# Scaling into SBUF, deviations for four batches, and a new division of work in a conditional adapter

## The chip, the cores and the metric

The kernel runs on one core of a Trainium2 chip. Five engines work side by side, each in the order of its own instructions: TensorE (PE in the profile; PEld is its weight load), VectorE (DVE), ScalarE (ACT), GpSimd (POOL) and SyncE (SP), which here only issues DMA transfers. The metric is the device time of one execution in microseconds, as the median of several runs; lower is better.

## The reference

For each of 128 batches b there are 128 rows of 512 numbers, x[b], and a language v = itok[b], one of 10. All is float32.

```python
w1, w2 = W1[language_ids], W2[language_ids]                 # 512 x 128, 128 x 512
h = relu(einsum('bsh,bha->bsa', x, w1) + b1[language_ids])
y = x + einsum('bsa,bah->bsh', h, w2) + b2[language_ids]
mean = y.mean(-1); var = ((y - mean) ** 2).mean(-1)
out = x + (y - mean) * rsqrt(var + 1e-5) * gamma[language_ids] + beta[language_ids]
```

## The kernel before

A batch is one tile of 128 rows x 512. W2 and the rows of beta, gamma and b2, spread over 128 partitions, stay in SBUF for all languages, and so does W1 in a tile `w1`. Each batch passes through these steps (functions of the same names):

- TensorE turns the four 128 x 128 blocks of x into PSUM (`transpose_x`), and ScalarE copies them to SBUF (`copy_xT`). For some batches ("F" in `TURNS`) x is loaded once more in blocks of 32 columns (`load_blocks`, four transfers), W1 likewise in rows that fit (`load_rows`, four transfers), and VectorE turns the blocks (`turn_blocks`); such a batch needs neither `transpose_x` nor `copy_xT`.
- W1 of the batch's language is copied by ScalarE from `w1` into a tile of its own (`stage_w1`); for "F" and "w" batches it comes by DMA.
- `down` (four matmuls of the program, eight instructions in the trace), `relu` on ScalarE, `up` into a PSUM tile `py`.
- x and b2 are added in one of several ways, by the batch's letter in `KINDS`. "P": GpSimd computes r = x + b2 (`add_b2`), and VectorE adds r to `py`. "E": ScalarE copies x into `py` first (`seed`), `up` accumulates onto it, and VectorE adds b2. A few batches at the beginning take other ways. The VectorE step is `residual`; it also writes the row sums.
- ScalarE squares (`square`), with the sum of squares as a by-product, and makes the negative mean (`scalar_means`) and the reciprocal root (`deviation`); VectorE refines the root in three small Newton steps (`rstd`). Means, roots and Newton steps are made for two batches at once. The root is written to a PSUM tile.
- VectorE scales: `scale` writes (py - mean) x gamma back to `py`, in PSUM. GpSimd has meanwhile written x + beta to the output tile o (`add_beta`). `finish`, the ending, computes o = py x rstd + o on VectorE.
- A pair of batches is stored by one transfer.

PSUM has five tiles for `py`. The output pool has 8 pairs. x is loaded in fours, in 4 buffers.

The order of each engine's instructions is fixed by the program. Batches 0 to 3 and the last five (from `E` on, and parts of the seven before them) are written out by hand. For all others a list `plan` holds each step with a time in units of one batch: the batch's number plus a number from a table (`BATCH` and `PAIR` in the steady part, `BATCH_EDGE` and `EDGE` outside it). The list is sorted by these times, and each engine gets its instructions in that order. In the steady part the letters repeat every 16 batches, a period:

```python
KINDS = 'EPPPPPEPEPPPEPPP'
TURNS = 'TTTTFTTTTwTTFTTT'
```

The lines that the profile names are: L330 `transpose_x`, L334 `copy_xT`, L302 `turn_blocks`, L321 `stage_w1`, L353 `down`, L361 `relu`, L367 and L375 `up`, L340 `add_b2`, L347 `add_beta`, L316 `seed`, L393 `residual`, L416 `square`, L426 `deviation`, L407 `scalar_means`, L430, L432 and L435 the Newton steps, L459 `scale`, L468 `finish`, L290 and L296 the loads of an "F" batch, L83 the load of x, L472 the store. L488 and L492 are beta's and b2's additions in the part written by hand, L519 and L523 two more of GpSimd's operations there, L553 and L559 its ending and its scaling into SBUF, and L220 an addition that splits the parameters at the start.

Of the kernel before, what the change touches and what calls it, by code (L numbers as in the profile page):

```python
# [16 lines left out]
P = 128  # L17
G = 4
EPS = 1e-5
# [3 lines left out]
U = 2  # L23
MIDDLE = 26
TURNED = 32
LAST = 4
KINDS = 'EPPPPPEPEPPPEPPP'
TURNS = 'TTTTFTTTTwTTFTTT'
SEEDED = 'E'
ON_GPSIMD = 'P'  # L30
BATCH = dict(turn=0.19, copy=0.16, r=-0.36, beta=-0.13, relu=1.26, w1=-0.77, up=2.66, load=-5.59, r_late=0.22)
BATCH_EDGE = dict(copy=0.2, r=0.05, r_late=1.05, beta=1.06, relu=1.3, w1=-0.6, up=2.5)
SEED = {'E': 1.69}
PAIR = dict(stat=0.22, square=0.34, means=1.98, root=1.9, scale0=3.03, n1=2.43, n2=3.115, n3=3.28, scale1=3.4, end0=3.67, end1=4.32)
EDGE = dict(stat=0.6, square=0.68, means=1.75, root=1.77, scale0=2.64, n1=2.65, n2=3.592, n3=3.62, scale1=3.64, end0=3.66, end1=4.66)
# [3 lines left out]
def cond_resid_kernel(ctx: ExitStack, tc: tile.TileContext, x, itok, W1, b1, W2, b2, gamma, beta, out):  # L39
# [41 lines left out]
    def load_x(g):  # L81
        t = xp.tile([P, G, H], FP, tag="x", name=f"x_{g}")
        keep(nc.sync.dma_start(out=t, in_=x[g * G : (g + 1) * G].rearrange("b s h -> s b h")))  # L83
        xs[g] = t

    def xb(b):
        return xs[b // G][:, b % G, :]

# [6 lines left out]
    x_0 = xp.tile([P, G, H], FP, tag="x", name="x_0")  # L95
    xs[0] = x_0

    def load_part(lo, hi, engine=nc.sync):
        dst = xs[lo // G][:, lo % G : lo % G + hi - lo, :]
        keep(engine.dma_start(out=dst, in_=x[lo:hi].rearrange("b s h -> s b h")))  # L100
# [85 lines left out]
    xs[1] = xp.tile([P, G, H], FP, tag="x", name="x_1")  # L186
# [6 lines left out]
    xs[2] = xp.tile([P, G, H], FP, tag="x", name="x_2")  # L193
# [6 lines left out]
    xs[3] = xp.tile([P, G, H], FP, tag="x", name="x_3")  # L200
# [8 lines left out]
    xs[4] = xp.tile([P, G, H], FP, tag="x", name="x_4")  # L209
# [55 lines left out]
    def b2_by_matmul(b):  # L265
        return b in (0, 1) or b >= B - 2

    def kind(b):
        return KINDS[b % len(KINDS)] if MIDDLE <= b < B - LAST else "-"

    def turn(b):
        return TURNS[b % len(TURNS)] if TURNED <= b < B - LAST - 2 else "-"

    def seeded(b):
        return kind(b) in SEEDED

    def b2_on_gpsimd(b):
        return kind(b) in ON_GPSIMD or kind(b) == "-" and not b2_by_matmul(b) and not b2_by_vector(b)

    def b2_by_vector(b):  # L280
        return kind(b) == "-" and (b in (2, 3, 9, 13, 17, 21) or 24 <= b < B - 8 and (b % 16 in (1, 6, 11) or b % 32 == 30))
# [36 lines left out]
    def stage_w1(b):  # L318
        w1s[b] = wp.tile([P, KC, A], FP, tag="w1s", name=f"w1s_{b}")
        src = w1.rearrange("p l k a -> p (l k a)")[:, bass.ds(lid(b, ET.Activation) * (KC * A), KC * A)]  # L320
        keep(nc.scalar.copy(w1s[b].rearrange("p k a -> p (k a)"), src))  # L321
# [20 lines left out]
    def add_beta(b):  # L342
        g, j = divmod(b, 2)
        if j == 0:
            os[g] = op.tile([P, 2, H], FP, tag="o", name=f"o_{g}")
        v = lid(b, ET.Pool)
        keep(nc.gpsimd.tensor_tensor(os[g][:, j, :], xb(b), beta_b[:, bass.ds(v * H, H)], ALU.add))  # L347
# [30 lines left out]
    def col(tiles, b):  # L378

        return tiles[b // 2][:, b % 2 : b % 2 + 1]  # L380
# [5 lines left out]

    def residual(b):
# [4 lines left out]
        keep(  # L392
            nc.vector.scalar_tensor_tensor(ys[b], ys[b], 1.0, r, ALU.mult, ALU.add, accum_out=sum_of(b))  # L393
        )
# [14 lines left out]
    def square(b):  # L409

        g, j = divmod(b, 2)
        if j == 0:
            ssqs[g] = st.tile([P, 2], FP, tag="ssq", name=f"ssq_{g}")
        sq = tp.tile([P, H], FP, tag="sq", name=f"sq_{b}", bufs=1)
        keep(
            nc.scalar.activation(  # L416
                sq, ys[b], AF.Square, bias=col(sums, b), scale=-float(H), accum_out=col(ssqs, b)
            )
        )
# [5 lines left out]
    def root(ssq, t):  # L425
        keep(nc.scalar.activation(t, ssq, AF.Abs_reciprocal_sqrt, bias=eps, scale=1.0 / H3))  # L426
# [12 lines left out]
    def of_pair(g):  # L439
        if g not in parts_of:  # L440
            parts_of[g] = p_s.tile([P, 2], FP, tag="s", name=f"root_{g}"), st.tile([P, 2], FP, tag="part", name=f"part_{g}")
        return parts_of[g]

    def deviation(g):
        root(ssqs[g], of_pair(g)[0])

    def rstd(g, n):
        t, u = of_pair(g)
        if n < 3:
            newton(n, ssqs[g], t, u)  # L450
        else:
            rstds[g] = st.tile([P, 2], FP, tag="rstd", name=f"rstd_{g}")
            newton_3(rstds[g], t, u)
            del ssqs[g], parts_of[g]

    def scale(b):
        v = lid(b, ET.DVE)
        keep(
            nc.vector.scalar_tensor_tensor(  # L459
                ys[b], ys[b], col(nmeans, b), gamma_b[:, bass.ds(v * H, H)], ALU.add, ALU.mult  # L460
            )
        )

    def finish(b):
        g, j = divmod(b, 2)
        o = os[g][:, j, :]
        keep(
            nc.vector.scalar_tensor_tensor(o, ys[b], rstds[g][:, j : j + 1], o, ALU.mult, ALU.add)  # L468
        )
# [178 lines left out]
    def at(when, step, *args):  # L648
        plan.append((when, len(plan), step, args))

    for b in range(B):
        when = BATCH_EDGE if kind(b) == "-" else BATCH
        if b >= 20 and b % G == 0:
            at((11 if b == 20 else b - 7) - 0.01, load_x, b // G)
# [4 lines left out]
        if turn(b) in "Fw":  # L659
            at(b + BATCH["load"] - 1, lid, b, ET.SP)  # L660
            at(b + BATCH["load"], load_rows if turn(b) == "F" else load_late, b)
        if turn(b) == "F":
            at(b + BATCH["load"], load_blocks, b)
            at(b + BATCH["turn"], turn_blocks, b)
        elif 5 <= b <= E - 2:
            at(b, transpose_x, b)
            at(b + when["copy"], copy_xT, b)
        if 4 <= b <= E - 3:
            at(b + (when["r"] if seeded(b) else when["r_late"]), add_b2, b)
            at(b + when["beta"], add_beta, b)  # L670
            at(b + 1.1, down, b)
            at(b + when["relu"], relu, b)
        if seeded(b):
            at(b + SEED[kind(b)], seed, b)
        if FIRST <= b <= E - 1 and turn(b) not in "Fw":
            at(b + when["w1"], stage_w1, b)
        if 2 <= b <= E - 4:
            at(b + when["up"], up, b)

    begun = [(step, n) for n in (E - 7, E - 6, E - 5) for step in (vector_b2, residual, square)]  # L680
    begun += [(scalar_means, E // 2 - 3), (deviation, E // 2 - 3), (scale, E - 7), (rstd, E // 2 - 3, 1)]

    def at_pair(g, when, step, *args):
        if g < E // 2 - 3 or (step, *args) in begun:
            at(2 * g + 3 + when, step, *args)

    for g in range(E // 2 - 1):
        b = 2 * g
        when = EDGE if "-" in (kind(b), kind(b + 2)) else PAIR
        for j in (0, 1):  # L690
            at_pair(g, j + when["stat"] - 0.01, vector_b2, b + j)
            at_pair(g, j + when["stat"], residual, b + j)
            at_pair(g, j + when["square"], square, b + j)
        at_pair(g, when["means"], scalar_means, g)
        at_pair(g, when["root"], deviation, g)
        if b % G == 0 and on(b + G):
            at_pair(g, when["end0"] + 0.001, lid, b + G, ET.DVE)
        for n in (1, 2, 3):
            at_pair(g, when[f"n{n}"], rstd, g, n)
        for j in (0, 1):  # L700
            at_pair(g, when[f"scale{j}"], scale, b + j)
            at_pair(g, when[f"end{j}"], finish, b + j)
        at_pair(g, when["end1"] + 0.001, store, g)
# [192 lines left out]
```

## Time and profile before

| | |
|---|---|
| median of 3 runs | 300.83 us (300.44 to 301.05) |
| profiled execution | 301.23 us |
| its span | 298.8 us |
| mean granted TensorE clock | 0.997 |
| busy share of the span | TensorE 97%, VectorE 97%, ScalarE 93%, GpSimd 93% |
| DMA | 85.48 MB moved, mean 286 GB/s |

The span reaches from the first to the last instruction of the profiled execution. Busy time counts where at least one instruction of an engine is recorded. On ScalarE, VectorE and GpSimd the records of neighbours overlap, so that the price of an instruction in a row of instructions is the distance from its start to the next one's start, which is shorter than its own record.

### The profile page before, as it was taken

What the parts mean: (1) busy time and instruction counts of PE and PEld (TensorE: products, weight loads), DVE (VectorE), ACT (ScalarE), POOL (GpSimd) and SP (SyncE); (2) the same over time, 40 slices, a digit from 0 to 9 for tenths busy, and PEclk for the clock granted to TensorE, in tenths of its full rate; (3) what the DMA queues carried; (4) which work ended last, traced back from release to release, by engine and by line L of the source; (5) the groups of instructions that cost most, each with busy time, mean ns of one, the idle gap of its engine ahead of it and who ended that gap; (6) DMA issues with size and microseconds to landing.
All of it is one profiled execution on the core that took longest, in us unless ns stands there. A gap on an engine that the chain in (4) does not pass through costs nothing.

```text
span 298.8 us, 7251 instructions
## 1 busy us (share of the span) xinstructions
PE 290.7 (97%) x1783; PEld 214.7 (72%) x1783; DVE 288.9 (97%) x775; ACT 277.2 (93%) x766; POOL 277.4 (93%) x233
## 2 busy tenths in 40 slices
PE   7899999999999999999999999999999999999993
PEld 3758777777777777777777777777777777777761
DVE  6989999999999999999999999999999999999995
ACT  5868789999999999999999999999999999999983
POOL 1299998999999999999999999999999999999962
PEclk9999999999999999999999999999999999999998
DMA  6999999996799697988888887898988698894715
GB/s 233 369 393 370 342 329 396 400 325 212 270 297 328 169 378 218 321 316 284 277 280 295 275 283 256 281 300 224 356 256 269 233 313 301 250 349 163 237 73 219
DMA packets 61195, 85.48 MB, mean 286 GB/s; under 512 B 3641, under 2 KB 25156, under 8 KB 61154
## 3 DMA queue, kind: packets, MB, share of 16 engines
q1 hardware_dynamic: 61094, 84.97, 85.1%
q8 instruction: 15, 0.25, 0.3%
q14 instruction: 26, 0.21, 0.2%
q10 hardware_dynamic: 60, 0.05, 0.1%
HBM read 51.45 MB, written 33.55 MB: 284 GB/s over the span
## 4 chain that ended last, share of the span: by engine, by line
PE 81%; DVE 6%; ACT 4%; DMA 3%; issue 3%; SPq 1%; DVEq 0%; POOL 0%; ACTq 0%; POOLq 0%
PE ph L353 33%; PE py L375 26%; PE pxT L330 15%; PE py L367 7%; DMA w<-in_L_cond_W_dram 3%; DVE py L393 2%; ACT sq L416 1%; DVE o L553 1%; DVE py L459 1%; ACT w1s L321 1%; ACT xT L334 1%; SPq L173 1%; DVE n L559 0%; ACT hT L361 0%; ACT root L426 0%
## 5 line engine op out<-in xcount | busy, mean ns | idle before, releaser
L347 POOL TENSOR_TENSOR o<-x,beta_b 128x512 f32<-128x512 f32 x121 | 155.8, 1306 | 12.9 <-DVE beta_b L259 11.6
L353 PE MATMUL ph<-xT,w1s 128*128 128x128 f32 x1024 | 136.4, 276 | 0.1
L353 PEld LDWEIGHTS ph<-xT,w1s 128*128 128x128 f32 x1024 | 125.0, 192 | 8.7 <-ACT hT L361 7.0
L340 POOL TENSOR_TENSOR r<-x,b_b 128x512 f32<-128x512 f32 x89 | 116.1, 1305 | 0.0
L375 PE MATMUL py<-w,hT 128*128 x208 | 106.7, 595 | 0.7 <-DMA w<-in_L_cond_W_dram 0.7
L330 PEld LDWEIGHTS pxT<-ident,x 128*128 128x128 f32 x468 | 60.4, 150 | 60.6 <-issue 41.6
L459 DVE SCALAR_TENSOR_TENSOR py<-py,nmean,gamma_b 128x512 f32<-128x512 f32 x124 | 93.3, 753 | 0.0
L468 DVE SCALAR_TENSOR_TENSOR o<-py,rstd,o 128x512 f32<-128x512 f32 x116 | 86.8, 748 | 0.0
L416 ACT ACTIVATE sq<-py,sum 128x512 f32<-128x512 f32 x124 | 85.6, 690 | 0.7 <-DVE rstd L435 0.2
L334 ACT COPY xT<-pxT 128x512 f32<-128x512 f32 x117 | 67.8, 580 | 6.0 <-PE pxT L330 5.8
L330 PE MATMUL pxT<-ident,x 128*128 128x128 f32 x468 | 71.2, 275 | 0.9 <-ACT gamma_b L244 0.7
L393 DVE SCALAR_TENSOR_TENSOR py<-py,r 128x512 f32<-128x512 f32 x94 | 64.9, 690 | 1.4
L321 ACT COPY w1s<-w 128x512 f32 x91 | 56.7, 623 | 0.0
L361 ACT ACTIVATE hT<-ph,b1T 128x128 f32<-128x128 f32 x128 | 47.6, 372 | 5.1 <-PE ph L353 3.4
L375 PEld LDWEIGHTS py<-w,hT 128*128 128x128 f32 x208 | 31.7, 192 | 2.1 <-DMA w<-in_L_cond_W_dram 1.2
L416 ACT ACTIVATION_READ_ACCUMULATOR sq<-py,sum 128x1 f32 x124 | 25.9, 209 | 0.0
L367 PE MATMUL py<-w,hT 128*128 x48 | 25.3, 610 | 0.0
L393 DVE SCALAR_TENSOR_TENSOR py<-py,b_b 128x512 f32<-128x512 f32 x24 | 16.6, 693 | 1.5 <-PE py L367 1.4
L426 ACT ACTIVATE root<-ssq,eps 128x2 f32<-128x2 f32 x62 | 16.5, 266 | 1.5
L316 ACT COPY py<-x 128x512 f32<-128x512 f32 x24 | 14.4, 599 | 0.0
L393 DVE DVE_READ_ACCUMULATOR py<-py,r 128x1 f32 x94 | 13.2, 140 | 0.0
L407 ACT ACTIVATE nmean<-sum 128x2 f32<-128x2 f32 x61 | 11.7, 192 | 0.0
(79 smaller groups left out, 139.8 us busy)
## 6 DMA issues: line engine op xcount, KB each, us to landing
out_dram<-o SPq DMA_DIRECT2D x62, 512.0 KB, 4.0
x<-in_x_dram SPq DMA_DIRECT2D x27, 1024.0 KB, 7.7
w1s<-in_L_cond_W_dram SPq DMA_DIRECT2D x26, 256.0 KB, 7.3
x<-in_x_dram SPq DMA_DIRECT2D x10, 512.0 KB, 6.0
w1s<-in_L_cond_W_dram SPq DMA_DIRECT2D x44, 64.0 KB, 3.2
x<-in_x_dram SPq DMA_DIRECT2D x44, 64.0 KB, 2.1
w<-in_L_cond_W_dram SPq DMA_DIRECT2D x4, 640.0 KB, 8.1
w<-in_L_cond_W_dram SPq DMA_DIRECT2D x1, 1792.0 KB, 10.2
```

What stands on the lines that cost most here:

```text
L321: keep(nc.scalar.copy(w1s[b].rearrange("p k a -> p (k a)"), src))
L330: keep(nc.tensor.transpose(pxs[b][:, k, :], cols, ident))
L334: keep(nc.scalar.copy(xT[b], pxs.pop(b)))
L340: keep(nc.gpsimd.tensor_tensor(rs[b], xb(b), b2_b[:, bass.ds(v * H, H)], ALU.add))
L347: keep(nc.gpsimd.tensor_tensor(os[g][:, j, :], xb(b), beta_b[:, bass.ds(v * H, H)], ALU.add))
L353: nc.tensor.matmul(phs[b], lhsT=w1s[b][:, k, :], rhs=xT_of(b, k), start=(k == 0), stop=(k == KC - 1))
L361: keep(nc.scalar.activation(hT[b], phs.pop(b), AF.Relu, bias=b1T[:, bass.ds(lid(b, ET.Activation), 1)]))
L375: keep(nc.tensor.matmul(ys[b], lhsT=hT[b], rhs=w2[:, bass.ds(v * H, H)], start=not m, stop=True))
L393: nc.vector.scalar_tensor_tensor(ys[b], ys[b], 1.0, r, ALU.mult, ALU.add, accum_out=sum_of(b))
L416: nc.scalar.activation(sq, ys[b], AF.Square, bias=col(sums, b), scale=-float(H), accum_out=col(ssqs, b))
L459: nc.vector.scalar_tensor_tensor(ys[b], ys[b], col(nmeans, b), gamma_b[:, bass.ds(v * H, H)], ALU.add, ALU.mult)
L468: nc.vector.scalar_tensor_tensor(o, ys[b], rstds[g][:, j : j + 1], o, ALU.mult, ALU.add)
```

## The change

The steps stay the same, and six things change.

1. `scale` writes its result for batches 8 to 111 (`QUADS`) into an SBUF tile of a new pool `n_pool` with 7 buffers, and `finish` reads it from there. `py` is free after `scale`.
2. For the same batches root and Newton steps are made for four batches at once.
3. x is loaded in pairs, in 8 buffers; the output pool has 6 pairs instead of 8.
4. In the steady part (now batches 32 to 111) 3 of 16 batches are turned by VectorE instead of 2, 8 of 16 are seeded instead of 4, and none loads W1 alone by DMA.
5. For 5 of 16 batches ("c" in `TURNS`) GpSimd copies W1 in place of ScalarE.
6. Every batch and step has its own time in a table `STEPS` (32 numbers for the beginning, 16 that repeat, 16 for the end), and `X_STEPS` has one for each load of x.

```diff
+X = 2
+QUADS = range(8, 112)
-KINDS = 'EPPPPPEPEPPPEPPP'
-TURNS = 'TTTTFTTTTwTTFTTT'
+KINDS = ('MMDDPPPPPDPPPDPPPDPPPDPPPPPPEPPP', 'EPEPPEEEPPEPEPEP', 'ESPEEPPPEPPPPPMM')
+TURNS = ('TTTTTTTTTTTTTTTTTTTTTTTTTTTTTTTT', 'cTFTTcTcFTTccTFT', 'TTccFccccTTTTTTT')
+STEPS = {
...
+    "n3": (
+        (2.89, 0, 4.81, 0, 6.26, 0, 5.6, 0, 9.15, 0, 0, 0, 9.02, 0, 0, 0, 8.63, 0, 0, 0, 8.44, 0, 0, 0, 8.92, 0, 0, 0, 7.95, 0, 0, 0,),
...
-    xp = ctx.enter_context(tc.tile_pool(name="xp", bufs=4))
+    xp = ctx.enter_context(tc.tile_pool(name="xp", bufs=8))
-    op = ctx.enter_context(tc.tile_pool(name="op", bufs=8))
+    op = ctx.enter_context(tc.tile_pool(name="op", bufs=6))
+    n_pool = ctx.enter_context(tc.tile_pool(name="n_pool", bufs=7))
...
     def stage_w1(b):
         w1s[b] = wp.tile([P, KC, A], FP, tag="w1s", name=f"w1s_{b}")
-        src = w1.rearrange("p l k a -> p (l k a)")[:, bass.ds(lid(b, ET.Activation) * (KC * A), KC * A)]
-        keep(nc.scalar.copy(w1s[b].rearrange("p k a -> p (k a)"), src))
+        gpsimd = turn(b) == "c"
+        v = lid(b, ET.Pool if gpsimd else ET.Activation)
+        src = w1.rearrange("p l k a -> p (l k a)")[:, bass.ds(v * (KC * A), KC * A)]
+        dst = w1s[b].rearrange("p k a -> p (k a)")
+        keep(nc.gpsimd.tensor_copy(dst, src) if gpsimd else nc.scalar.copy(dst, src))
...
     def of_set(g):
         if g not in parts_of:
-            parts_of[g] = p_s.tile([P, 2], FP, tag="s", name=f"root_{g}"), st.tile([P, 2], FP, tag="part", name=f"part_{g}")
+            n = size(2 * g)
+            parts_of[g] = p_s.tile([P, n], FP, tag="s", name=f"root_{g}"), st.tile([P, n], FP, tag="part", name=f"part_{g}")
...
     def scale(b):
         v = lid(b, ET.DVE)
+        if b in QUADS:
+            ns[b] = n_pool.tile([P, H], FP, tag="n", name=f"scaled_{b}")
         keep(
             nc.vector.scalar_tensor_tensor(
-                ys[b], ys[b], col(nmeans, b), gamma_b[:, bass.ds(v * H, H)], ALU.add, ALU.mult
+                ns.get(b, ys[b]), ys[b], col(nmeans, b), gamma_b[:, bass.ds(v * H, H)], ALU.add, ALU.mult
...
     def finish(b):
-        g, j = divmod(b, 2)
-        o = os[g][:, j, :]
+        o = os[b // 2][:, b % 2, :]
+        r = rstds[square_set(b)][:, b % size(b) : b % size(b) + 1]
         keep(
-            nc.vector.scalar_tensor_tensor(o, ys[b], rstds[g][:, j : j + 1], o, ALU.mult, ALU.add)
+            nc.vector.scalar_tensor_tensor(o, ns.pop(b, ys[b]), r, o, ALU.mult, ALU.add)
```

Counted over the whole program, the instructions that change in number are: `transpose_x` 117 to 112 batches, `turn_blocks` 11 to 16, `add_b2` on GpSimd in the plan 89 to 68, `seed` 24 to 46 (one of them from r), W1 copies 91 on ScalarE to 61 on ScalarE and 31 on GpSimd, sets of root and Newton steps 62 to 36, loads of x in the plan 27 to 54, loads of W1 alone behind batch 16 from 9 to 3.

VectorE in the steady part, in the order of the program: before, one pair's scaling, Newton steps and endings (`py` is the PSUM tile, `part`, `root` and `rstd` the Newton steps' tiles, `o` the output tile).

```order
L459 SCALAR_TENSOR_TENSOR py_2859<-py_2859,nmean_2962,gamma_b 128x512
L432 SCALAR_TENSOR_TENSOR part_2960<-part_2960,root_2959 128x2
L393 SCALAR_TENSOR_TENSOR py_2999,sum_2987<-py_2999,r_2882 128x512
L435 SCALAR_TENSOR_TENSOR rstd_3040<-part_2960,root_2959 128x2
L459 ISA
L459 SCALAR_TENSOR_TENSOR py_2905<-py_2905,nmean_2962,gamma_b 128x512
L468 SCALAR_TENSOR_TENSOR o_2740<-py_2859,rstd_3040,o_2740 128x512
L393 SCALAR_TENSOR_TENSOR py_3045,sum_3070<-py_3045,r_2925 128x512
L468 SCALAR_TENSOR_TENSOR o_2740<-py_2905,rstd_3040,o_2740 128x512
```

VectorE in the steady part of the changed kernel (`scaled` is the new SBUF tile; L593 is `scale`, L602 `finish`, L514 `residual`, L550, L552 and L555 the Newton steps).

```order
L550 SCALAR_TENSOR_TENSOR part_2933<-ssq_2809,root_2932 128x4
L593 ISA
L593 SCALAR_TENSOR_TENSOR scaled_2936<-py_2887,nmean_2909,gamma_b 128x512
L552 SCALAR_TENSOR_TENSOR part_2933<-part_2933,root_2932 128x4
L593 ISA
L593 SCALAR_TENSOR_TENSOR scaled_2953<-py_2791,nmean_2909,gamma_b 128x512
L555 SCALAR_TENSOR_TENSOR rstd_2982<-part_2933,root_2932 128x4
L514 SCALAR_TENSOR_TENSOR py_2918,sum_2930<-py_2918,r_2881 128x512
L602 SCALAR_TENSOR_TENSOR o_2786<-scaled_2867,rstd_2982,o_2786 128x512
L602 SCALAR_TENSOR_TENSOR o_2786<-scaled_2911,rstd_2982,o_2786 128x512
```

The Newton steps work on four columns instead of two, scaling goes into a tile that is not its source, and the ending takes both of its large inputs, `scaled` and `o`, from SBUF; two endings stand next to each other.

GpSimd in the steady part, before: beta's and b2's additions (`o` and `r`) alone.

```order
L347 ISA
L347 TENSOR_TENSOR o_3001<-x_2708,beta_b 128x512
L340 ISA
L340 TENSOR_TENSOR r_3068<-x_2708,b_b 128x512
L347 ISA
L347 TENSOR_TENSOR o_3086<-x_2708,beta_b 128x512
L340 ISA
L340 TENSOR_TENSOR r_3102<-x_2708,b_b 128x512
```

GpSimd in the changed kernel, near the beginning of the steady part (L438 is the copy of W1, L464 `add_beta`, L457 `add_b2`).

```order
L438 ISA
L438 COPY w1s_1750<-w_94 128x512
L464 ISA
L464 TENSOR_TENSOR o_1760<-x_1258,beta_b 128x512
L457 ISA
L457 TENSOR_TENSOR r_1807<-x_1562,b_b 128x512
L438 ISA
L438 COPY w1s_1816<-w_94 128x512
L464 ISA
L464 TENSOR_TENSOR o_1760<-x_1258,beta_b 128x512
```

Copies of W1 now stand between the additions, and fewer of the additions are of b2.

More of the change, by code (lines that the diff above doesn't have):

```diff
@@ L262, in cond_resid_kernel, with of, kind, turn @@
     phs, pxs, sums = {}, {}, {}
-    def b2_by_matmul(b):
[L266 to L272, printed above, removed]
+    steady = len(KINDS[1])
+    closing = B - len(KINDS[2])
+    def of(parts, b):
+        if b < len(parts[0]):
+            return parts[0][b]
+        return parts[1][b % steady] if b < closing else parts[2][b - closing]
+    def kind(b):
+        return of(KINDS, b)
+    def turn(b):
+        return of(TURNS, b)
+    def b2_by_matmul(b):
+        return kind(b) == "M"
     def seeded(b):
@@ L673, in cond_resid_kernel @@
+            at(when("beta", b), add_beta, b)
+            at(when("down", b), down, b)
+            at(when("relu", b), relu, b)
         if seeded(b):
-            at(b + SEED[kind(b)], seed, b)
-        if FIRST <= b <= E - 1 and turn(b) not in "Fw":
-            at(b + when["w1"], stage_w1, b)
+            at(when("seed", b), seed, b)
+        if FIRST <= b <= E - 1 and turn(b) != "F":
+            at(when("w1", b), stage_w1, b)
         if 2 <= b <= E - 4:
-            at(b + when["up"], up, b)
@@ L698, in cond_resid_kernel @@
[L698 to L703, printed above, removed]
+        for n in (b, b + 1):
+            if kind(n) == "S":
+                at_pair(g, when("sum", n), total, n)
+            else:
+                if b2_by_vector(n):
+                    at_pair(g, when("vb2", n), vector_b2, n)
+                at_pair(g, when("stat", n), residual, n)
+            at_pair(g, when("square", n), square, n)
@@ new lines, in cond_resid_kernel @@
+        at_pair(g, when("means", b), scalar_means, g)
+        if first_of(b) == b:
+            at_pair(g, when("root", b), deviation, g)
+            for n in (1, 2, 3):
+                at_pair(g, when(f"n{n}", b), rstd, g, n)
+        for n in (b, b + 1):
+            at_pair(g, when("scale", n), scale, n)
+            at_pair(g, when("end", n), finish, n)
+        if b % G == 0 and on(b + G):
+            at_pair(g, when("scale", b) + 0.001, lid, b + G, ET.DVE)
+        at_pair(g, when("store", b), store, g)
```

143 lines of the change are left out of this document (85 added, 58 removed), and 74 rows, old and new, of the table STEPS.

## Prediction

> **What bounds the kernel now.** First the totals of the page, then the chain that ended last, then the pace of one period of 16 batches, engine by engine.
>
> ```profile
> span 298.8 us, 7251 instructions
> PE 290.7 (97%) x1783; PEld 214.7 (72%) x1783; DVE 288.9 (97%) x775; ACT 277.2 (93%) x766; POOL 277.4 (93%) x233
> ```
>
> No engine stands out: four of them are busy for 93% or more. The profiled execution took 301.23 us, 2.4 us more than its span, and lies 0.4 us above the median of the runs, 300.83 us. The chain in order of time shows where its work lies (columns: start, length, what):
>
> ```profile
> 6.24 10.20 DMA w<-in_L_cond_W_dram
> ...
> 16.49 1.13 PE py L375 x2
> ...
> 161.32 0.86 PE py L375 x2
> 162.18 0.44 PE pxT L330 x4
> 162.62 0.89 PE ph L353 x8
> ...
> 267.67 0.79 ACT sq L416 x2
> ```
>
> Up to 16.5 us everything waits for W2. From there to about 267 us the chain is TensorE; then it passes through ScalarE and VectorE. A batch costs TensorE 0.44 (turning x) + 0.89 (down) + 0.86 (up) = 2.19 us, and a batch whose x VectorE turns 1.75 us. In the steady part 2 of 16 are of that kind: 14 x 2.19 + 2 x 1.75 = 34.2 us a period.
>
> ```profile
> 88.72 0.70 DVE L302 STREAM_TRANSPOSE xT<-x 128x512 f32<-128x512 f32 x1
> ...
> 123.31 0.70 DVE L302 STREAM_TRANSPOSE xT<-x 128x512 f32<-128x512 f32 x1
> ```
>
> ```profile
> L347 POOL TENSOR_TENSOR o<-x,beta_b 128x512 f32<-128x512 f32 x121 | 155.8, 1306 | 12.9 <-DVE beta_b L259 11.6
> ...
> L340 POOL TENSOR_TENSOR r<-x,b_b 128x512 f32<-128x512 f32 x89 | 116.1, 1305 | 0.0
> ```
>
> ```profile
> 13.07 4.98 POOL L347 TENSOR_TENSOR o<-x,beta_b 128x512 f32<-128x512 f32 x4 [11.61 <-DVE beta_b L259]
> ...
> 283.07 2.54 POOL L488 TENSOR_TENSOR o<-x,beta_b 128x512 f32<-128x512 f32 x2
> 286.57 1.27 POOL L519 TENSOR_TENSOR n<-n,gamma_b 128x512 f32<-128x512 f32 x1 [0.96 <-ACT n L504]
> ```
>
> The two VectorE turns (first fence; then two groups with count, busy us and mean ns, and three rows of GpSimd in order of time) are one period apart (batches 36 and 52): 34.59 us, slightly over TensorE's own 34.2. GpSimd explains the rest. Its additions follow one another without a gap from 13.07 to 285.6 us. Between the first row and the row at 283.07 stand 121 + 89 + 10 - 2 = 218 of them (the 10 are the hand-written ones at the end), so one costs (283.07 - 13.07) / 218 = 1.2385 us from start to start, less than the 1306 ns of a record since neighbours overlap. A period has 16 beta and 12 b2 additions: 28 x 1.2385 = 34.7 us, the measured pace. So GpSimd sets the pace, TensorE stands 0.5 us a period behind it, and an edit must relieve both.
>
> **The change part by part.** Start-to-start prices for ScalarE and VectorE come from neighbouring rows:
>
> ```profile
> 160.63 0.56 ACT L334 COPY xT<-pxT 128x512 f32<-128x512 f32 x1
> 161.09 0.61 ACT L321 COPY w1s<-w 128x512 f32 x1
> 161.61 0.36 ACT L361 ACTIVATE hT<-ph,b1T 128x128 f32<-128x128 f32 x1
> ...
> 164.73 0.27 ACT L426 ACTIVATE root<-ssq,eps 128x2 f32<-128x2 f32 x1
> 164.93 0.19 ACT L407 ACTIVATE nmean<-sum 128x2 f32<-128x2 f32 x1
> ...
> 166.93 0.60 ACT L316 COPY py<-x 128x512 f32<-128x512 f32 x1
> 167.45 0.60 ACT L334 COPY xT<-pxT 128x512 f32<-128x512 f32 x1
> ```
>
> ```profile
> 158.08 0.70 DVE L302 STREAM_TRANSPOSE xT<-x 128x512 f32<-128x512 f32 x1
> 158.70 0.67 DVE L393 SCALAR_TENSOR_TENSOR py<-py,r 128x512 f32<-128x512 f32 x1
> ...
> 162.02 0.76 DVE L459 SCALAR_TENSOR_TENSOR py<-py,nmean,gamma_b 128x512 f32<-128x512 f32 x1
> 162.68 0.15 DVE L432 SCALAR_TENSOR_TENSOR part<-part,root 128x2 f32<-128x2 f32 x1
> 162.74 0.69 DVE L393 SCALAR_TENSOR_TENSOR py<-py,r 128x512 f32<-128x512 f32 x1
> 163.35 0.15 DVE L435 SCALAR_TENSOR_TENSOR rstd<-part,root 128x2 f32<-128x2 f32 x1
> ...
> 164.09 0.75 DVE L468 SCALAR_TENSOR_TENSOR o<-py,rstd,o 128x512 f32<-128x512 f32 x1
> 164.75 0.69 DVE L393 SCALAR_TENSOR_TENSOR py<-py,r 128x512 f32<-128x512 f32 x1
> ```
>
> *More batches turned by VectorE* (11 to 16 in all, 3 of 16). TensorE loses 5 x 0.44 = 2.2 us; ScalarE 5 copies of xT, 5 x 0.46 = 2.3. VectorE gains 5 x 0.62 = 3.1. A period of TensorE becomes 13 x 2.19 + 3 x 1.75 = 33.7 us.
>
> *Seeds* (24 to 46). ScalarE gains 22 x 0.52 = 11.4 us; GpSimd loses 21 b2 additions (89 to 68), 21 x 1.2385 = 26.0.
>
> *W1 copied by GpSimd* (31 copies; ScalarE's go from 91 to 61). ScalarE loses 30 x 0.52 = 15.6. No row shows a GpSimd copy. It has one input, half of what an addition reads; the nearest rows are the addition of half width and the full one:
>
> ```profile
> L393 DVE SCALAR_TENSOR_TENSOR py<-py,r 128x512 f32<-128x512 f32 x94 | 64.9, 690 | 1.4
> ...
> L559 DVE SCALAR_TENSOR_TENSOR n<-py,nmean,gamma_b 128x512 f32<-128x512 f32 x2 | 1.5, 750 | 0.0
> ...
> L523 POOL TENSOR_TENSOR o<-n,o 128x256 f32<-128x256 f32 x2 | 1.4, 726 | 0.1
> ...
> L220 DVE TENSOR_TENSOR rows<-rows 30x512 f32<-30x512 f32 x1 | 0.7, 681 | 0.1
> ```
>
> The half-width addition reads as many elements as the copy would: 0.73 less the overlap of 0.07 is 0.66 us. The upper bound is 1.24. I take 0.66, because the two inputs of an addition look like its limit (half the elements read, 0.58 us saved). GpSimd then has 199 x 1.2385 + 31 x 0.66 = 267.0 us of work from 13.07 us on, against 272.5 now: 5.5 us less, 33.0 us a period. The copies break even at 26.0 / 31 = 0.84 us. The Trainium skill, GPSIMD Engine Reference, section "Performance versus the Vector engine", measures 769 ns for 512 elements in a tight one-input loop; by that the copies would take 23.8 us and GpSimd would gain 2.2 us, not 5.5.
>
> *Root and Newton for four batches* (62 sets to 36). ScalarE loses 26 x 0.20 = 5.2 us, VectorE 78 x 0.065 = 5.1. A batch now waits longer for its deviation, which PSUM no longer pays, since the scaled value sits in SBUF (7 buffers; about 3 to 4 batches pass between scaling and ending). What pays is the output tiles: by the step tables they live 9 to 10 batches from beta's addition to the store's landing, and 6 pairs hold 12 instead of 16. If that cover is gone, GpSimd's beta addition waits for a store's landing.
>
> *Scaling into SBUF.* Scaling itself costs the same (750 ns into SBUF in the L559 row; 0.76 in the row at 162.02). The ending keeps 0.66 us if only its source is new: a VectorE addition with both inputs in SBUF took 681 ns, beside 690 for PSUM and SBUF, but GpSimd was not adding then.
>
> *x in pairs, loads and stores moved.* The bytes of x stay. 27 issues of x more at 0.41 us and five turned batches more, four W1 and four x issues each, fall on SyncE:
>
> ```profile
> 163.00 2.02 SPq L296 DMA_DIRECT2D w1s<-in_L_cond_W_dram  x4
> 165.12 1.79 SPq L290 DMA_DIRECT2D x<-in_x_dram  x4
> ...
> 167.51 0.41 SPq L83 DMA_DIRECT2D x<-in_x_dram  x1
> ```
>
> That is 3 x 3.8 + 8 x 0.41 + 8 stores at about the same price = 18 us of a 34 us period, behind which a load or store can queue but not fall back for good. I cost it at nothing; a pair arriving late would hold one turn of x.
>
> Sums: ScalarE 11.4 - 15.6 - 2.3 - 5.2 = 11.7 us less. VectorE 3.1 - 5.1 = 2.0 less; its period is 16 x (0.66 + 0.61 + 0.66) + 4 x 3 x 0.065 + 3 x 0.62 = 33.5 us. So TensorE at 33.7 comes next, VectorE right behind it, GpSimd at 33.0. With four engines this close I give back 1% for waits, about what TensorE loses now: 34.1 instead of 34.6. Over some 6 periods that is 3 us; with none given back 5.4, with all of it zero. The execution of 301.2 becomes 298.2; less the 0.4 to the median, 297.8, rounded to 298.0.
>
> **The rivals.**
>
> *VectorE and GpSimd get in each other's way.* All VectorE operations of full size beside GpSimd's additions now read at most one operand from SBUF, the other from PSUM; 104 endings will read both (scaled and o) from SBUF. No row shows such an operation while GpSimd runs, so the trace neither excludes nor shows a collision. Against it: GpSimd's spacing is 1.2385 on average beside a VectorE that is 97% busy, without gaps. If each ending stops GpSimd for its full 0.66 us, GpSimd has 267.0 + 104 x 0.66 = 335.6 us of work; 13.1 in front, 13.3 behind (298.8 - 285.5) and the 2.4 give 364 us. If half of it stops, 330. It decides from about 0.05 us an ending (5.5 / 104). Where VectorE waits too, the time is at the upper end. The Trainium skill, SBUF — State Buffer, section "Who interferes with whom", states just this: a VectorE instruction with two SBUF inputs contends with a GpSimd instruction that reads SBUF, and whoever comes second is fully blocked. The present trace agrees only in that operations with one SBUF input don't disturb GpSimd.
>
> *GpSimd's copy costs as much as its addition.* At 1.24 us: 199 x 1.2385 + 31 x 1.2385 = 284.9, so 313.7 us; it decides from 0.84.
>
> *Longer holding.* Six output pairs or late pairs of x make GpSimd wait; one addition a period lost is 1.24 x 6 = 7 us, some 305.
>
> *Nothing.* TensorE and VectorE lose to each other what GpSimd gives: 300.8.
>
> **How the numbers follow.** About 0.2% can be told from no change here, 0.6 us. The forecast gets 0.48: the sums of four engines all fall. The collision gets 0.30: it has the largest price, and the trace holds neither a row for it nor one against it. The dear copy 0.12, the longer holding 0.05, nothing 0.05. Faster 0.48, same 0.05, slower 0.47. The forecast's own range is 295.5 (all 5.4 us) to 300.2. To hold 8 in 10 the range must take in the dear copy and the longer holding (to 314) and the lower half of the collision, where it stops under half of each ending: to 335.
>
> **What would show it.** Right: GpSimd's copies near 0.66 us apart, its additions still 1.24 apart beside the endings, VectorE turns of one period (now batches 34 and 50) about 34.1 us apart. Wrong: spacing of GpSimd's additions, or records of the ending, grown where they overlap (collision); copies above 0.84; GpSimd idle before beta's addition, released by a store (holding).

## The result, and the profile after

The changed kernel takes 357.79 us (median of 6 runs, 357.19 to 358.15), the kernel before 300.94 us in the same comparison: a ratio of 1.1892, with a 95% interval of 1.1874 to 1.191. Here and below, a ratio and its interval leave out executions in which the chip was in its slower state, while medians and ranges take in all of them, so a ratio need not be the quotient of two medians. Forecast were 298.0 us. The forecast's sign was wrong; the rival "VectorE and GpSimd get in each other's way", with its price of 364 us, is what happened.

First the totals of the page after:

```profile
span 356.2 us, 7280 instructions
PE 312.5 (88%) x1763; PEld 217.2 (61%) x1763; DVE 344.8 (97%) x700; ACT 271.2 (76%) x729; POOL 312.6 (88%) x243
```

TensorE and ScalarE have fallen to 88% and 76%: they wait now. VectorE is at 97% as before, but of a span that is 57.4 us longer, although it has 75 instructions fewer. GpSimd is busy for 312.6 us, against 277.4 before, although its work was to shrink by 5.5. So instructions on these two have grown. The groups, shapes apart (count, then busy us and mean ns, then idle time in front):

```profile
L464 POOL TENSOR_TENSOR o<-x,beta_b 128x512 f32<-128x512 f32 x121 | 181.7, 1521 | 17.0 <-DVE beta_b L365 12.7 <-DMA out_dram<-o 4.3
L602 DVE SCALAR_TENSOR_TENSOR o<-scaled,rstd,o 128x512 f32<-128x512 f32 x104 | 133.9, 1312 | 0.7
L457 POOL TENSOR_TENSOR r<-x,b_b 128x512 f32<-128x512 f32 x68 | 96.7, 1429 | 3.3 <-DVE part L550 1.0 <-DVE py L514 0.9 <-DVE rstd L555 0.7
L593 DVE SCALAR_TENSOR_TENSOR scaled<-py,nmean,gamma_b 128x512 f32<-128x512 f32 x104 | 75.6, 737 | 1.3 <-ACT nmean L528 0.8 <-ACT sq L536 0.3 <-issue 0.2
L438 POOL COPY w1s<-w 128x512 f32 x31 | 21.1, 688 | 10.4 <-PE ph L470 9.7 <-DVE xT L416 0.7
L602 DVE SCALAR_TENSOR_TENSOR o<-py,rstd,o 128x512 f32<-128x512 f32 x12 | 8.8, 748 | 0.4
```

The two L602 rows are the same line with the same shape. Where the first operand still comes from PSUM (12 times) an ending takes 748 ns, where it is `scaled` in SBUF (104 times) 1312: 104 x 0.564 = 58.7 us, the size of the whole loss. GpSimd's additions have grown too, from 1306 ns to 1521 and 1429. Scaling itself (L593) costs no more for writing to SBUF: 737 ns, against 0.76 us in the prediction's row at 162.02. The instructions of L602 one by one, min/median/max:

```profile
L602 DVE SCALAR_TENSOR_TENSOR o<-scaled,rstd,o x104: 735/1148/1865, 47.7 to 320.4; 128x512 f32<-128x512 f32 x104
L602 DVE SCALAR_TENSOR_TENSOR o<-py,rstd,o x12: 742/750/753, 23.9 to 329.9; 128x512 f32<-128x512 f32 x12
```

The PSUM form never leaves 742 to 753 ns. The SBUF form can be as short (735), but ranges to 1865: it depends on what runs beside it. The order in time shows on what. GpSimd first, then VectorE, in the same stretch:

```profile
151.42 3.41 POOL L464 TENSOR_TENSOR o<-x,beta_b 128x512 f32<-128x512 f32 x2
154.79 1.27 POOL L457 TENSOR_TENSOR r<-x,b_b 128x512 f32<-128x512 f32 x1
156.02 1.72 POOL L464 TENSOR_TENSOR o<-x,beta_b 128x512 f32<-128x512 f32 x1
157.69 1.17 POOL L438 COPY w1s<-w 128x512 f32 x2
```

```profile
152.55 1.15 DVE L602 SCALAR_TENSOR_TENSOR o<-scaled,rstd,o 128x512 f32<-128x512 f32 x1
153.62 1.40 DVE L593 SCALAR_TENSOR_TENSOR scaled<-py,nmean,gamma_b 128x512 f32<-128x512 f32 x2
...
155.55 1.07 DVE L602 SCALAR_TENSOR_TENSOR o<-scaled,rstd,o 128x512 f32<-128x512 f32 x1
156.54 0.69 DVE L514 SCALAR_TENSOR_TENSOR py<-py,r 128x512 f32<-128x512 f32 x1
```

The addition from 154.79 on is under way when the ending at 155.55 begins: it keeps its 1.27 us, and the ending takes 1.07 instead of 0.75. The addition at 156.02 begins while that ending still runs (to 156.6): it takes 1.72. The two additions from 151.42 on, 3.41 us together, meet the ending at 152.55, which takes 1.15. Whoever comes second pays, sometimes one engine and sometimes the other.

The whole trace bears this out, and more sharply than these rows. Of the 104 endings 85 begin while an addition is running, and 80 of the 85 end 0.55 us after that addition ends, however early in it they began. Additions meet 93 times an ending that is already running; 90 of these end 1.13 us after the ending does, and their record is 1.72 us in the median. Additions that no earlier ending meets take 1.26 to 1.29 us. So the second one does not go on more slowly: it stands until the first is through, and then needs most of its own time (0.55 of an ending's 0.75, 1.13 of an addition's 1.27). The remaining 0.2 and 0.14 us of the two records overlap with the other engine's work.

The pace, by the VectorE turns of batches 34, 50 and 66, one period apart:

```profile
98.89 0.69 DVE L416 STREAM_TRANSPOSE xT<-x 128x512 f32<-128x512 f32 x1
...
144.70 0.70 DVE L416 STREAM_TRANSPOSE xT<-x 128x512 f32<-128x512 f32 x1
...
185.55 0.70 DVE L416 STREAM_TRANSPOSE xT<-x 128x512 f32<-128x512 f32 x1
```

The first period lasts 45.81 us, the second 40.85; before it was 34.59. The first one holds 18 endings, with 23.97 us, and the second 16. The busy time of each engine in the second one, and below it VectorE's in the endings alone (L602):

```profile
144.70:185.55 40.85, 36.63 (x212) 25.36 (x212) 40.76 (x80) 32.84 (x89) 38.88 (x30) 1.00 0.74 244
...
144.70:185.55 40.85, 18.51 (x16) 1.00 0.74 244
```

VectorE (third value) fills 40.76 of 40.85 us: it is the bound, with GpSimd at 38.88. The 16 endings take 18.51 us there; 16 of 748 ns would take 11.97. The 6.54 us between them cover the 6.26 us by which the period has grown. The granted clock (1.00, third from the right) has no part in it. Set against before, with batch b of before at 88.72 + (b - 36) x 34.59 / 16, batch 50 is turned 25.7 us later than before (144.70 against 119.0), batch 98 (at 267.23) 44.4 us later than 222.8, and the end comes 57.4 us later.

### The profile page after: what moved, and what is told of

It reads as the page before. It is cut to its first block, busy times and chain, and to the rows that moved or that the text cites. A ratio compares the mean times of both kernels' runs of the same rounds, so it can differ in the third digit from the quotient of the medians.

```text
span 356.2 us, 7280 instructions
## 1 busy us (share of the span) xinstructions
PE 312.5 (88%) x1763; PEld 217.2 (61%) x1763; DVE 344.8 (97%) x700; ACT 271.2 (76%) x729; POOL 312.6 (88%) x243
## 5 line engine op out<-in xcount | busy, mean ns | idle before, releaser
L464 POOL TENSOR_TENSOR o<-x,beta_b 128x512 f32<-128x512 f32 x121 | 181.7, 1521 | 17.0 <-DVE beta_b L365 12.7
L602 DVE SCALAR_TENSOR_TENSOR o<-scaled,rstd,o 128x512 f32<-128x512 f32 x104 | 133.9, 1312 | 0.7
L536 ACT ACTIVATE sq<-py,sum 128x512 f32<-128x512 f32 x124 | 85.0, 685 | 38.8 <-DVE py L514 33.5
L457 POOL TENSOR_TENSOR r<-x,b_b 128x512 f32<-128x512 f32 x68 | 96.7, 1429 | 3.3 <-DVE part L550 1.0
L447 PEld LDWEIGHTS pxT<-ident,x 128*128 128x128 f32 x448 | 57.4, 153 | 66.5 <-ACT xT L451 33.5
L593 DVE SCALAR_TENSOR_TENSOR scaled<-py,nmean,gamma_b 128x512 f32<-128x512 f32 x104 | 75.6, 737 | 1.3 <-ACT nmean L528 0.8
L514 DVE SCALAR_TENSOR_TENSOR py<-py,r 128x512 f32<-128x512 f32 x72 | 49.2, 686 | 1.3 <-PE py L492 1.3
L438 ACT COPY w1s<-w 128x512 f32 x61 | 37.8, 624 | 1.9 <-issue 1.2
L514 DVE SCALAR_TENSOR_TENSOR py<-py,b_b 128x512 f32<-128x512 f32 x45 | 30.9, 686 | 0.1
L492 PEld LDWEIGHTS py<-w,hT 128*128 128x128 f32 x164 | 25.5, 195 | 8.2 <-DVE scaled L593 3.0
L438 POOL COPY w1s<-w 128x512 f32 x31 | 21.1, 688 | 10.4 <-PE ph L470 9.7
L430 ACT COPY py<-x 128x512 f32<-128x512 f32 x45 | 26.8, 596 | 1.9 <-DVE scaled L593 1.8
L528 ACT ACTIVATE nmean<-sum 128x2 f32<-128x2 f32 x61 | 12.6, 206 | 11.7 <-DVE py L514 10.4
L484 PEld LDWEIGHTS py<-w,hT 128*128 128x128 f32 x92 | 14.1, 194 | 1.2 <-ACT py L430 0.6
```

Source lines behind the costliest of these rows:

```text
L438: keep(nc.gpsimd.tensor_copy(dst, src) if gpsimd else nc.scalar.copy(dst, src))
L447: keep(nc.tensor.transpose(pxs[b][:, k, :], cols, ident))
L457: keep(nc.gpsimd.tensor_tensor(rs[b], xb(b), b2_b[:, bass.ds(v * H, H)], ALU.add))
L484: keep(nc.tensor.matmul(ys[b], lhsT=hT[b], rhs=cols, start=False, stop=True, skip_group_check=True))
L492: keep(nc.tensor.matmul(ys[b], lhsT=hT[b], rhs=w2[:, bass.ds(v * H, H)], start=not m, stop=True))
L536: nc.scalar.activation(sq, ys[b], AF.Square, bias=col(sums, b), scale=-float(H), accum_out=ssqs[square_set(b)][:, b % size(b) : b % size(b ...
```

## The experiments

Theory A is the collision of endings with two SBUF inputs and GpSimd's reads; B is the new order and longer holding of tiles; C an ending that is slow by itself when its source is in SBUF; D, formed after the first runs, is A for some 47 us and the order for the other 10.

**The endings' second operand from PSUM.** In the changed kernel, the 104 endings add a column of zeros in PSUM instead of `o`, so x + beta is left out of these outputs. The column lies in a PSUM tile `held`, in which the roots of all batches are now written too; order and other tiles stay.

```diff
+    held = p_s.tile([P, 64], FP, name="held")
+    flat = held[:, 63:64]
...
-            parts_of[g] = p_s.tile([P, n], FP, tag="s", name=f"root_{g}"), st.tile([P, n], FP, tag="part", name=f"part_{g}")
+            parts_of[g] = held[:, 0:n], st.tile([P, n], FP, tag="part", name=f"part_{g}")
...
-            nc.vector.scalar_tensor_tensor(o, ns.pop(b, ys[b]), r, o, ALU.mult, ALU.add)
+            nc.vector.scalar_tensor_tensor(
+                o, ns.pop(b, ys[b]), r, flat.to_broadcast([P, H]) if b in QUADS else o, ALU.mult, ALU.add
+            )
```

> The changed kernel, whose 104 endings take their second large operand from a PSUM column instead of the output tile in SBUF (so x + beta is left out of these outputs); all else, the order and the GpSimd additions, stays. Theory A (an ending with both inputs in SBUF and a reading GpSimd addition shut each other out): endings back to records of about 0.75 us and additions to 1.30, the time about 298 us, 295 to 303. Theory B (the new order, the four-batch wait, fewer output tiles or more transfers cost the time): 340 us or more, as the changed kernel.

311.03 us (306.85 to 312.02), 1.0278 times before, interval 1.0189 to 1.0368. Neither expectation is met. Its groups:

```profile
L467 POOL TENSOR_TENSOR o<-x,beta_b 128x512 f32<-128x512 f32 x121 | 152.4, 1281 | 24.2 <-DVE beta_b L368 13.0 <-DMA out_dram<-o 11.1
L605 DVE SCALAR_TENSOR_TENSOR o<-scaled,rstd,held 128x512 f32<-128x512 f32 x104 | 74.6, 745 | 1.4 <-ACT held L549 0.5 <-issue 0.3
L441 POOL COPY w1s<-w 128x512 f32 x31 | 18.8, 615 | 0.0
```

The ending is back at 745 ns with `scaled` still in SBUF, the addition at 1281: it is not the new source but the second SBUF input. 46.8 of the 57 us go. The other 10 (6 to 11, by the single runs) do not, and their sign too is against the forecast. The shared tile makes ScalarE wait for endings for 3.6 us in all, so this run alone can't tell whether the 10 come from it. What waits now shows in the first row, with 11.1 us for stores, and in the chain of waits:

```profile
216.87 1.31 POOL o L467 x2
218.18 7.55 DMA x<-in_x_dram
225.75 2.28 DMA x<-in_x_dram
228.21 0.09 DVE xT L419
```

The chain stands on loads of x for 9.8 us, and what it releases then is VectorE's turn (L419).

**Scaling into SBUF alone.** In the kernel before, only this one part of the change, with 3 tiles `scaled` instead of 7:

```diff
+    n_pool = ctx.enter_context(tc.tile_pool(name="n_pool", bufs=3))
...
+        if b in QUADS:
+            ns[b] = n_pool.tile([P, H], FP, tag="n", name=f"scaled_{b}")
...
-                ys[b], ys[b], col(nmeans, b), gamma_b[:, bass.ds(v * H, H)], ALU.add, ALU.mult
+                ns.get(b, ys[b]), ys[b], col(nmeans, b), gamma_b[:, bass.ds(v * H, H)], ALU.add, ALU.mult
...
-            nc.vector.scalar_tensor_tensor(o, ys[b], rstds[g][:, j : j + 1], o, ALU.mult, ALU.add)
+            nc.vector.scalar_tensor_tensor(o, ns.pop(b, ys[b]), rstds[g][:, j : j + 1], o, ALU.mult, ALU.add)
```

> The kernel before with one part alone: scaling for batches 8 to 111 goes into an SBUF tile (3 buffers), and the ending reads it from there; order, mix and buffers are those of before. Theory A: 340 to 360 us, endings with records of 1.1 to 1.3 us, additions of up to 1.75. Theory B: 299 to 303 us.

348.0 us (346.65 to 348.12), 1.1556 times before, interval 1.1527 to 1.1585.

```profile
L349 POOL TENSOR_TENSOR o<-x,beta_b 128x512 f32<-128x512 f32 x121 | 177.0, 1474 | 12.9 <-DVE beta_b L261 12.7 <-DMA out_dram<-o 0.2
L342 POOL TENSOR_TENSOR r<-x,b_b 128x512 f32<-128x512 f32 x89 | 134.7, 1513 | 3.9 <-DVE py L395 3.9
L474 DVE SCALAR_TENSOR_TENSOR o<-scaled,rstd,o 128x512 f32<-128x512 f32 x104 | 127.0, 1221 | 0.0
```

This part alone, in the old order, loses 47.4 us. Endings and additions grow as in the full change, and here 103 of the 104 endings end 0.55 us after the addition in which they began. What one experiment takes away (46.8) is about what the other adds.

**Half of the endings.** As the first experiment, but the zeros only in odd batches.

```diff
...
+                o, ns.pop(b, ys[b]), r, flat.to_broadcast([P, H]) if b in QUADS and b % 2 else o, ALU.mult, ALU.add
```

> The changed kernel with the PSUM operand in the endings of odd batches only (x + beta left out there), so 52 endings keep both inputs in SBUF. Theory A: about 320 us (VectorE's period 33.5 + 8 x 0.55 = 37.9 us instead of 34.1, six periods and a half), 315 to 328; long endings only among those of even batches. Theory B: 340 or more.

326.99 us (326.12 to 327.5), 1.0865 times before, interval 1.0838 to 1.0891.

```profile
L605 DVE SCALAR_TENSOR_TENSOR o<-scaled,rstd,o 128x512 f32<-128x512 f32 x52 | 63.2, 1234 | 0.7
L605 DVE SCALAR_TENSOR_TENSOR o<-scaled,rstd,held 128x512 f32<-128x512 f32 x52 | 37.9, 737 | 0.0
```

Side by side in one program, only the form with two SBUF inputs grows. With 0, 52 and 104 of them the times are 311.0, 327.0 and 357.8: the first half costs 16, of 52 x 0.497 = 25.8 us added to VectorE; the second costs 31. This fits the first half having met slack: VectorE is busy for 93% of the span in the first experiment, and for 96% here.

**The prices by themselves.** A kernel of its own, which computes nothing of the reference: 12 endings in a row beside nothing, beside additions (first operand in PSUM, then in SBUF), beside copies and beside memsets of GpSimd.

```python
for _ in range(N):
    keep(nc.vector.scalar_tensor_tensor(t, first, r, second, ALU.mult, ALU.add))
```

> The prices by themselves, in stretches behind one another, none of it the reference's computation: 12 endings (128 x 512, both inputs in SBUF) alone; 8 GpSimd additions alone; both with the ending's first input in PSUM; both with its two inputs in SBUF; endings beside GpSimd copies; endings beside GpSimd memsets. Theory A: start to start 0.66 us alone, beside copies over 0.9, beside additions 1.2 or more with additions at 1.7, beside memsets 0.66 (the memset reads nothing), and with PSUM 0.66 and 1.24. Theory C (an ending with both inputs in SBUF is slow by itself): 1.1 us or more also alone.

One profile. First the groups (`d_two`: both in SBUF, beside additions; `d_one`: one in PSUM, beside additions; `d_copy`, `d_set`: both in SBUF, beside copies and memsets), then VectorE's rows in order of time:

```profile
L71 POOL TENSOR_TENSOR p_two<-xa,xb 128x512 f32<-128x512 f32 x14 | 21.6, 1543 | 1.0
L64 DVE SCALAR_TENSOR_TENSOR d_two<-n,r,o 128x512 f32<-128x512 f32 x12 | 19.8, 1647 | 0.4
...
L64 DVE SCALAR_TENSOR_TENSOR d_copy<-n,r,o 128x512 f32<-128x512 f32 x12 | 11.9, 991 | 0.4
...
L71 POOL TENSOR_TENSOR p_alone<-xa,xb 128x512 f32<-128x512 f32 x8 | 10.1, 1260 | 0.5
L64 DVE SCALAR_TENSOR_TENSOR d_alone<-n,r,o 128x512 f32<-128x512 f32 x12 | 9.0, 752 | 0.4
L64 DVE SCALAR_TENSOR_TENSOR d_set<-n,r,o 128x512 f32<-128x512 f32 x12 | 9.0, 752 | 0.4
L64 DVE SCALAR_TENSOR_TENSOR d_one<-y,r,o 128x512 f32<-128x512 f32 x12 | 9.0, 750 | 0.4
```

```profile
25.38 9.39 DVE L64 SCALAR_TENSOR_TENSOR d_one<-y,r,o 128x512 f32<-128x512 f32 x12
36.17 20.15 DVE L64 SCALAR_TENSOR_TENSOR d_two<-n,r,o 128x512 f32<-128x512 f32 x12
58.93 12.28 DVE L64 SCALAR_TENSOR_TENSOR d_copy<-n,r,o 128x512 f32<-128x512 f32 x12
```

This settles C: alone, an ending with both inputs in SBUF takes 752 ns. An instruction of GpSimd that only writes doesn't disturb it (752), one that reads one tile makes it 991, one that reads two makes it 1647. In a row, an ending takes 9.39 / 12 = 0.78 us beside additions if one input is in PSUM, 20.15 / 12 = 1.68 if both are in SBUF. (Alone it takes as much, 11 of them 8.63 us, and so more than the 0.66 of the kernel before; why was not looked into.) The Trainium skill, SBUF — State Buffer, section "Who interferes with whom", states the contention for two SBUF inputs and a GpSimd instruction that reads; the rows agree. The full block of the second one, which the prediction took from there, shows as well. An ending and an addition by turns take 1.68 us together, which is the 0.55 and the 1.13 of the changed kernel one behind the other. Their whole records one behind the other would take 0.78 + 10.63 / 8 = 2.11 (the 8 undisturbed additions took 10.63 us), so the beginning or end of a record is not part of the block.

**One large input, without the help of PSUM.** The endings as a multiplication of `scaled` by the deviation alone, in a form with an accumulated sum, so that x + beta is left out and the order and the holding of tiles stay:

```diff
+        if b in QUADS:
+            junk = st.tile([P, 1], FP, tag="junk", name=f"junk_{b}", bufs=2)
+            keep(nc.vector.tensor_scalar(o, ns.pop(b), r, 0.0, ALU.mult, ALU.add, accum_out=junk))
+            return
```

> The changed kernel, whose 104 endings are scaled x rstd alone, with one large input from SBUF and no PSUM operand (x + beta left out of these outputs; a by-product of row sums keeps it a plain one-input operation), so that the root need not wait for an ending as in the first experiment. Theory A with nothing else wrong: about 298 us. Theory D (the collision costs some 47 us, and the new order with its few output tiles and late transfers the other 10): 306 to 311 us, with GpSimd waiting for stores.

310.6 us (308.15 to 311.74), 1.0304 times before, interval 1.0256 to 1.0352: the first experiment again, with other means. The roots have tiles of their own again. So the 10 us that stay do not come from the column of zeros or from the tile that it shared.

**One more pair of output tiles**, on top of the last (7 pairs, and 5 tiles `scaled` instead of 7 to make room):

```diff
-    op = ctx.enter_context(tc.tile_pool(name="op", bufs=6))
-    n_pool = ctx.enter_context(tc.tile_pool(name="n_pool", bufs=7))
+    op = ctx.enter_context(tc.tile_pool(name="op", bufs=7))
+    n_pool = ctx.enter_context(tc.tile_pool(name="n_pool", bufs=5))
```

> The same with 7 pairs of output tiles instead of 6 (and 5 scaled tiles instead of 7, to make room). If the output tiles are what holds theory D's 10 us: 300 to 304 us and hardly a wait of GpSimd for a store. If it is late loads or the order of GpSimd's own work: as the run before, within 2 us.

309.18 us (304.99 to 310.19), 1.021 times before, interval 1.0145 to 1.0276, which overlaps the last one's: by itself inconclusive, and nearer to the second expectation than to the first. GpSimd's wait for stores (us in all, times, longest), first without the pair, then with it:

```profile
POOL o L464 <- DMA out_dram<-o: 13.8, 8, 3.7
```

```profile
POOL o L464 <- DMA out_dram<-o: 6.6, 7, 1.4
```

**Loads of the turned batches earlier**, on top of that: two entries of the step table for the loads of W1 and x of these batches, from -2.67 and -2.68 to -5.

```diff
-        (0, 0, -2.67, 0, 0, 0, 0, 0, -5, 0, 0, 0, 0, 0, -2.68, 0,),
+        (0, 0, -5, 0, 0, 0, 0, 0, -5, 0, 0, 0, 0, 0, -5, 0,),
```

> The run with 7 output pairs and one-input endings (x + beta left out of them), whose W1 and x for batches turned by VectorE are loaded 5 units ahead in all three places of the period instead of 2.67, 5 and 2.68. If loads that land late behind SyncE's other work hold the rest of theory D's 10 us: 300 to 305 us, no wait of a VectorE turn for a load. If not: 308 to 310.

305.33 us (304.44 to 305.98), 1.0158 times before, interval 1.0141 to 1.0175, apart from that of one input alone: tiles and loads together give back some 5 us. It is not apart from the interval of the run just before, so the share of each is open. One period of it, from the turn of batch 50 to that of 66, and the totals of its page:

```profile
121.56:155.43 33.87, 33.87 (x215) 25.58 (x215) 33.77 (x96) 32.77 (x91) 33.14 (x31) 1.00 0.93 297
```

```profile
PE 290.4 (96%) x1763; PEld 212.9 (70%) x1763; DVE 287.0 (95%) x804; ACT 267.9 (89%) x729; POOL 269.4 (89%) x243
```

TensorE (first busy value) fills the period: 33.87 us, a little under the forecast 34.1 and 0.7 under before. Batch 98 is turned at 223.24 us, nearly level with the 222.8 of before, although batch 50 was 2.6 us late; from there to the end it takes 3.4 us longer than before. What holds the start and the closing was not taken apart.

**Five batches of 16 seeded in the kernel before**, to see whether GpSimd alone sets its pace (one b2 addition a period less). In a period of the kernel before, TensorE and GpSimd (first and last busy value) are both busy all the time:

```profile
88.72:123.31 34.59, 34.59 (x218) 25.87 (x217) 34.22 (x93) 34.04 (x96) 34.59 (x29) 1.00 0.87 281
```

```diff
-KINDS = 'EPPPPPEPEPPPEPPP'
+KINDS = 'EPPPEPEPEPPPEPPP'
```

> The kernel before with one more batch of 16 seeded (5 instead of 4), the reference's computation whole. If GpSimd sets the pace of the kernel before: 33.4 us a period there instead of 34.7, TensorE's 34.2 next, 6 periods, so about 2.5 us less: 297.5 to 299.5. If TensorE sets it: 300.8.

302.95 us (302.77 to 303.39), 1.0081 times before, interval 1.0063 to 1.01. Slower, with GpSimd relieved, and under neither expectation. Groups of `up` (plain, then seeded), and pieces of the chain:

```profile
L378 PE MATMUL py<-w,hT 128*128 x196 | 100.4, 594 | 0.0
...
L370 PE MATMUL py<-w,hT 128*128 x60 | 32.2, 618 | 0.0
```

```profile
166.41 0.86 PE py L378 x2
...
168.76 1.12 PE py L370 x2
```

From 88 to 124 us the chain is TensorE throughout, and a seeded `up` (L370) takes up to 1.12 us in it where a plain one takes 0.86: seeds cost TensorE time. The period is 35.10 us, 0.51 longer than before. The longer records of `up` (10 of 618 ns a period, where before has 8 of 610) are only a part of that; the rest was not taken apart.

**Six of 16 with two W1 copies of GpSimd**, otherwise as the last:

```diff
-KINDS = 'EPPPPPEPEPPPEPPP'
-TURNS = 'TTTTFTTTTwTTFTTT'
+KINDS = 'EPPPEPEPEPEPEPPP'
+TURNS = 'TTTcFTTTTwTTFTTc'
```

> The kernel before with 6 of 16 batches seeded and W1 copied by GpSimd for 2 of 16, the reference's computation whole. GpSimd 33.4 us a period, ScalarE no fuller than before: 297.5 to 299.5 if GpSimd set the pace, 300.8 if TensorE did; above 301 if the two copies delay the batches behind them.

304.98 us (304.81 to 305.49), 1.0142 times before, interval 1.0121 to 1.0163: slower again by about as much. But its period, 34.99 us, is no longer than with five. Of what is added, 2.0 us lie at the end: from the last turn on VectorE it takes 39.4 us, where five seeds take 37.4.

**Seeds earlier**, with five seeds and then in the kernel before alone, so that ScalarE's copy is done well ahead of the matmul:

```diff
-SEED = {'E': 1.69}
+SEED = {'E': 1.3}
```

> The kernel before with 5 of 16 batches seeded, each seed placed ahead of one square more on ScalarE (1.3 instead of 1.69 units after its batch); the computation is whole. If a seed that comes late to its matmul is what made five seeds slower (0.96 us a seeded up, 0.86 a plain one): 298 to 300. If accumulating onto a seed costs TensorE that by itself: 302 to 303.5.

> The kernel before with its 4 seeds of 16 placed at 1.3 instead of 1.69 units; nothing else. If late seeds cost TensorE: 4 x 0.05 us a period less, 299 to 300.5. If not: 300.8, or more, since the PSUM tile is held for longer.

318.97 us (318.86 to 319.2), 1.0606 times before, interval 1.0591 to 1.062; and 314.57 us (314.42 to 314.88), 1.0456, interval 1.0442 to 1.0471. Neither fits a gain from early seeds. The group of seeded `up` in the kernel before and then in the second of these runs, and a wait of the second:

```profile
L367 PE MATMUL py<-w,hT 128*128 x48 | 25.3, 610 | 0.0
...
L367 PE MATMUL py<-w,hT 128*128 x48 | 24.6, 594 | 0.0
```

```profile
PE py L375 <- DVE part L430: 8.8, 17, 0.9
```

The stretch is gone (594 ns, like a plain one, against 610): it came from the seed landing just ahead. But a seeded PSUM tile is then held longer, and the plain `up` (L375) waits for VectorE, of which it needs nothing but a free tile. No version tried beats the kernel before.

## Why the prediction was wrong

- **The step that failed: "The ending keeps 0.66 us if only its source is new."** It was priced with a row in which GpSimd wasn't adding, as that sentence says itself. Beside GpSimd the ending takes 1312 ns, and with one input in PSUM 745, because it stands until GpSimd's addition is through. That is 47 of the 57 us. The spacing of GpSimd's additions, named against the collision, was no evidence: every operation of VectorE beside them read at most one operand from SBUF, so it could not have shown one. (Nor was it quite "without gaps": GpSimd waited once, 1.3 us at 47.7 for a store.) A price from a row that lacks the very condition should not have carried 0.48, with 0.30 for the collision.
- **The rival's price**, 364 us, came close to 357.8 with the payer mistaken, which is luck. It let GpSimd stop for 0.66 us an ending. Measured, both pay: VectorE 58.7 us over 104 endings, the additions 121 x 0.215 + 68 x 0.123 = 34.4 us in their records, or 0.33 us an ending; and since VectorE was the fuller one, it sets the pace (40.76 of 40.85 us).
- **"It decides from about 0.05 us an ending"** holds: the 0.33 us by which an ending delays GpSimd lies far beyond, and so does the 0.56 by which it grows itself.
- **The pace without the collision** was right: 34.1 forecast, 34.11 and 34.30 in two of the four periods of the first experiment (35.65 and 36.48 in the others), 33.87 where tiles and loads are there in time. TensorE's 33.7 came out as the next bound, and VectorE's 33.5 close behind as 33.77.
- **The sums** hold to within 2.5 us in the last version without the collision: VectorE's busy time is 1.9 us under before (forecast 2.0), ScalarE's 9.3 (forecast 11.7), GpSimd's 8.0 (forecast 5.5).
- **GpSimd's copy** at 0.66 us was right: records of 615 ns undisturbed, under the break-even of 0.84 and under the 769 ns of the prediction's other price. The rival of the dear copy falls.
- **"I cost it at nothing"**, of the work added to SyncE and of late pairs of x, was mis-sized. Six pairs of output tiles also cover less than the prediction had them cover (13.8 us of waits for stores). The chain stood 9.8 us on loads in the first experiment; tiles and earlier loads give back some 5 us together. Of the 10 us that remain without the collision, the other 4 to 5 lie in the start and the closing (2.6 and 3.4 us, less what the shorter periods win back), which the prediction summed as unchanged; what makes them is open.
- **"So GpSimd sets the pace"** was half right. With one addition a period less, the kernel before got 0.8% slower: TensorE, 0.5 us behind in the sum, was level in fact (busy for all of the 34.59 us, as GpSimd was), and the added seed made the period 0.51 us longer.

Not tried: an ending with x + beta kept and one input in PSUM beside this order of work. All versions without the collision leave x + beta out of 104 endings, so their times are no offer of a faster kernel, only a measure of what the collision costs.

## What to carry to other kernels

Before moving an operand of a VectorE instruction from PSUM to SBUF, count its SBUF inputs and look at what GpSimd does at that time: price it with a row in which both run, or measure that pair alone in a small kernel. A busy share does not show such a loss, since the wait is inside the record; compare mean and spread of one line's forms instead. And where four engines are busy for 34.0 to 34.6 of 34.59 us of a period, relieving one brought nothing here: the steps that feed the others have to be counted too.

## What was not expected of the hardware

- A VectorE instruction with two SBUF inputs went from 752 ns alone to 1647 beside GpSimd additions with two inputs, 991 beside its copies and 752 beside its memsets; the additions went from 1260 to 1543.
- The second one stands until the first is through: in the changed kernel 80 of the 85 endings that began during an addition ended 0.55 us after it, whether they began 0.1 or 1.1 us into it.
- With one input and an accumulated sum, VectorE's multiplication from SBUF to SBUF did not disturb GpSimd: 741 ns, with additions of 1282.
- A matmul that accumulates on a tile which ScalarE has just written takes longer (618 ns on average, 1.12 us for two at worst, against 594 and 0.86); written earlier, it does not.
